# Two levels of seven products in the routed first layers, and first-layer sums that stay in P1's bank and are restored by ScalarE

## The chip, the core and the metric

The kernel runs as one program on one core of a Trainium2 chip. The metric is the device time of one execution in microseconds (us). The kernel before has a median of 1692.92 us over 3 runs (1692.71 to 1692.92). TensorE multiplies matrices, VectorE and ScalarE work on rows of 128 partitions, GpSimd and SyncE (SP) here mostly issue DMAs.

## What is computed

The input x has 2 x 2048 rows of 512 values, in f32 throughout. A modulated linear layer makes z from x. Then z goes through a gated feed-forward layer with a hidden width of 2048: a shared one for all rows, and one of two experts, chosen for each row by its gate score. A row's other expert sees zeros, so that only its biases count.

```python
z = einsum('bsi,io->bso', x * ys[:, None, :], weight) * d[:, None, :]
top1 = argmax(softmax(z @ gate_w.T))
masked = z[None] * one_hot(top1, 2).T[:, :, None]
h = relu(einsum('end,edh->enh', masked, w1) + b1[:, None, :])
routing_output = (einsum('enh,ehd->end', h, w2) + b2[:, None, :]).sum(0)
shared = relu(z @ sw1 + sb1) @ sw2 + sb2
return x + routing_output + shared
```

## The kernel before

**Stages.** The program is one list of stages, and each engine works through its instructions in the order in which the program gives them. The modulation comes first (to about 123 us of the span). Then come four shared units of 1024 rows (loop at L1271), three routed units of 1024 rows that were gathered by expert, one routed unit of 512 rows (loop at L1311), and a last piece of 256 rows (from about 1640 us). A unit (`unit`, L714) has a first layer, 512 to 2048 with relu, and a second layer, 2048 to 512.

**First layer.** Both halves of rows, of inputs and of outputs make 2 x 2 blocks, which are multiplied with seven products in place of eight (Strassen-Winograd): P1 = A11 B11, P2 = A12 B21, P3 = S4 B22, P4 = A22 T4, P5 = S1 T1, P6 = S2 T2, P7 = S3 T3. A are blocks of weights and S their sums, B are blocks of rows and T their sums; T come from `z_sums` (L404), four VectorE operations of the whole width (T3 takes the place of B12). The outputs are h11 = P1+P2, h12 = P1+P6+P5+P3, h21 = P1+P6+P7+P4 and h22 = P1+P6+P7+P5. The loop over c runs 8 times, once for each pair of 128-wide output blocks; `product` (L763) is two matmuls of 128 x 512 in a routed or shared unit. In a pair: P1 goes to a bank and ScalarE copies it to s1 (L779); `last` adds P3 of the pair before to its P5 bank (L804); P6 goes to a bank of its own, and VectorE makes u2 = P6 + s1 (L784); P2 is added in P1's bank and ScalarE's relu reads it (L774); VectorE makes u3 = P7 + u2 (L791), h22 = P5 + u3 (L794) and h21 = P4 + u3 (L798). Banks come from two pools: "pa" and "po".

**Second layer.** `layer2_twice` (L891) uses seven products at two levels: seven calls of `seven` (L916), each of seven products of four 128 x 256 matmuls (L938). The 512-row unit uses one level (`layer2_once`, L827).

**Work put in between.** Hooks name places in a unit: ("in", c) is inside pair c, c behind it, "m0" to "m4" and ("n", step, i) lie in the second layer. `hosted` (L1055) computes a small group of 128 rows inside a routed unit, eight steps of a first part (phr, L1070, 1.75 us of TensorE) and a second (por, L1083). `put` (L1001) transposes finished outputs; `run_late` (L708) calls it step by step. `rows_of` (L391) transposes rows of z in the first shared unit.

**Sums of weights.** The blocks S of the weights are made on VectorE during the shared units and stored in DRAM for later units: for w1 of both experts 16 jobs of `job1` (L263), which load on GpSimd's queue and store to s1E on SP's; for sw2 and w2 twelve jobs of `split_twice` (L278), which load on GpSimd's queue and store on SP's (L293, L303), in pieces of 512 bytes. `split_hooks` (L371) gives 4, 3, 3 and 2 of these jobs to the four shared units. The first shared unit makes sums of sw1 as it goes (`made`, L525); `stored` (L1110) loads blocks and stored sums for a pair of a first layer, two pairs ahead, on SP's queue.

Of the kernel before, what the change touches and what calls it, by code (L numbers as in the profile page):

```python
# [16 lines left out]
def kernel(  # L17
# [36 lines left out]
    P = 128  # L54
# [57 lines left out]
    s1S = dram.tile([1, H2, P, 4, K2, P], F32, name="s1S")  # L112
    s2S = dram.tile([1, 4, P, H2, D // 2], F32, name="s2S")
    s1E = dram.tile([E, H2, P, 4, K2, P], F32, name="s1E")
    s2E = dram.tile([E, 4, P, H2, D // 2], F32, name="s2E")

    H4 = H2 // 2
    LV = ("A11", "A12", "A22", "S1", "S2", "S3", "S4")
    w2S = dram.tile([1, 7, P, 4, H4, P], F32, name="w2S")
    w2E = dram.tile([E, 7, P, 4, H4, P], F32, name="w2E")  # L120

# [31 lines left out]
    b2_sb = wpool.tile([P, D], F32, tag="w1", name="b2_sb")  # L153
    nc.scalar.dma_start(b2_sb[: E + 1, :], b2)
    load_xT(1)
    gate_sb = wpool.tile([P, E, D], F32, tag="w1", name="gate_sb")
# [106 lines left out]
    def job1(e, c):  # L263
        r = work.tile([P, KD, 2, P], F32, tag="cr", name="r1", bufs=2)
        for i in range(2):
            nc.gpsimd.dma_start(
                r[:, :, i, :], w1[e][:, ts(c + i * H2, P)].rearrange("(k p) h -> p k h", p=P)
            )

        def make():  # L270
            o = work.tile([P, 4, K2, P], F32, tag="zp", name="o1")
            lo, hi = slice(0, K2), slice(K2, KD)
            sums([o[:, i] for i in range(4)], r[:, lo, 0], r[:, hi, 0], r[:, lo, 1], r[:, hi, 1])
            nc.sync.dma_start(s1E[e, c], o)

        return make

    def split_twice(todo):  # L278


        def load(src, q, *_):
            r = wpool.tile([P, 4, D], F32, tag="w2", name="jobr")
            nc.gpsimd.dma_start(r, src.rearrange("(j k q p) d -> q p (j k) d", p=P, q=H4, k=2)[q])
            return r

        def group(l0, x, y):

            s2_, s3_, s1_, s4_ = (y[:, l0 : l0 + x(0, 0).shape[1], i] for i in range(4))
            sums((s1_, s2_, s3_, s4_), x(0, 0), x(1, 0), x(0, 1), x(1, 1))

        def keep(dst, q, l0, n, y):
            for i in range(4):
                nc.sync.dma_start(dst[l0 : l0 + n].rearrange("l p m q d -> q m p l d")[q, i], y[:, :, i])  # L293

        held = load(*todo[0])
        yield
        a, b = slice(0, D // 2), slice(D // 2, D)
        for i, (src, q, dst, store, then) in enumerate(todo):
            r = held
            S = wpool.tile([P, 4, 2, D // 2], F32, tag="w2", name="jobs")  # L300
            sums([S[:, i] for i in range(4)], r[:, 0:2, a], r[:, 2:4, a], r[:, 0:2, b], r[:, 2:4, b])
            for k in range(2):
                nc.sync.dma_start(store.rearrange("s p (k q) d -> q k p s d", q=H4)[q, k], S[:, :, k])  # L303
            yield
            for l in (0, 2):
                y = work.tile([P, 2, 4, P], F32, tag="cs", name="y", bufs=2)
                group(0, lambda k, m: S[:, l : l + 2, k, ts(m, P)], y)
                keep(dst, q, 3 + l, 2, y)
            if i + 1 < len(todo):
                held = load(*todo[i + 1])  # L310
            yield
            y = S.rearrange("p s k d -> p (s k d)")[:, : 12 * P].rearrange("p (l m d) -> p l m d", l=3, m=4)
            rj = r.rearrange("p (j k) d -> p j k d", k=2)
            group(0, lambda k, m: rj[:, :, k, ts(m, P)], y)
            group(2, lambda k, m: rj[:, 1:2, k, D // 2 + m * P : D // 2 + (m + 1) * P], y)
            keep(dst, q, 0, 3, y)
            if then:
                yield
                then(q, r)
            yield  # L320
# [32 lines left out]
    class Jobs:  # L353


        def __init__(self, jobs):
            self.jobs, self.make = jobs, None

        def step(self, more=True):
            make, self.make = self.make, (self.jobs.pop(0)() if self.jobs and more else None)  # L360
            if make:
                make()

    expert_jobs = Jobs([lambda e=e, c=c: job1(e, c) for e in range(E) for c in range(H2)])
    split_jobs = [(sw2, q, w2S[0], s2S[0], None) for q in range(H4)]
    for e in range(E):
        split_jobs += [
            (w2[e], q, w2E[e], s2E[e], lambda q, r, e=e: zeros_add(e, q, r)) for q in range(H4)
        ]

    def split_hooks(n):  # L371

        steps = split_twice([split_jobs.pop(0) for _ in range(n)])

        def step():
            for f in zero_late[:]:
                zero_late.remove(f)
                f()
            next(steps, None)

        hooks = {c: [step] for c in range(H2 - 1)}
        hooks.update({("in", c): [step] for c in range(H2 - 1)})
        return hooks
# [20 lines left out]
    def z_sums(W=T):  # L404
        z = [zslot(i, W) for i in range(7)]
        nc.vector.tensor_sub(z[T1], z[B12], z[B11])
        nc.vector.tensor_sub(z[T2], z[B22], z[T1])
        nc.vector.tensor_sub(z[B12], z[B22], z[B12])
        nc.vector.tensor_sub(z[T4], z[B21], z[T2])
# [115 lines left out]
    def made(c):  # L525

        w = wpool.tile([P, 14, P], F32, tag="w1", name=f"w1m_{c}")
        a21 = work.tile([P, K2, P], F32, tag="hs", name=f"a21_{c}", bufs=2)
        nc.sync.dma_start(w[:, 0:4, :], shared_a1(c))
        nc.sync.dma_start(w[:, 4:6, :], shared_a1(c + H2)[:, K2:, :])  # L530
        nc.sync.dma_start(a21, shared_a1(c + H2)[:, :K2, :])

        def make():
            sums([w[:, 6 + 2 * i : 8 + 2 * i] for i in range(4)], w[:, 0:2], w[:, 2:4], a21, w[:, 4:6])
            nc.gpsimd.dma_start(s1S[0, c].rearrange("p s k h -> p (s k) h"), w[:, 6:14])

        return w, make

    first = []
# [174 lines left out]
    def unit(name, W, src, bias, row, hooks, after):  # L714
# [6 lines left out]
        weights, a2, d2, ws, split = src  # L721
# [28 lines left out]
        last = None  # L750
        ws = list(ws) + [weights(c) for c in range(len(ws), 2)]
        for c in range(H2):
            if c == 0:
                ws[0][1]()
            if c + 1 < H2:
                ws[c + 1][1]()
            if len(ws) < min(c + 3, H2):
                ws.append(weights(c + 2))
            w = ws[c][0]

            def product(ps, wi, zi, start, stop, w=w):
                for k in range(K2):
                    nc.tensor.matmul(  # L763
# [5 lines left out]
            def temp(tag):  # L769
                return work.tile([P, W], F32, tag=tag, name=f"{tag}{name}_{c}", bufs=2)  # L770
# [9 lines left out]
            if last is not None:  # L780
                last()
# [609 lines left out]
```

## Time and profile before

| | |
|---|---|
| median of 3 runs | 1692.92 us |
| the profiled execution's time, its span | 1692.93 us, 1691.2 us |
| shared unit 0: first layer, second | 123 to 224 us, 224 to 308 us |
| shared units 1, 2, 3 end at | 497, 689, 876 us |
| routed units of 1024 rows: end at | 1095, 1310, 1522 us |
| routed unit of 512 rows, last piece: end at | 1640, 1691 us |
| DMA, whole run | 335.30 MB, mean 198 GB/s |

The groups of the first layers are the costliest of the page. "r" at the end of a name means routed, "s" shared; two forms are in one group where the 512-row unit's 256-wide tiles are counted too.

```profile
L763 PE MATMUL p1r<-zs_all,w1r 128*128 128x512 f32 (+1 forms) x256 | 106.7, 539 | 0.0
L763 PE MATMUL p5r<-zs_all,w1r 128*128 128x512 f32 (+1 forms) x256 | 106.6, 539 | 0.0
L763 PE MATMUL p1s<-zs_all,w1s 128*128 128x512 f32 x192 | 91.0, 596 | 0.2 <-DVE u3s L791 0.2
```

A row has line, engine and operation, output and inputs, shapes and count; then busy time in us and the mean of one in ns; then the engine's idle time ahead of the group and what ended it. P2 is counted with p1 and P3 with p5, since they share their banks. Rows of "PEld" are weight loads of TensorE, which overlap its matmuls.

### The profile page before, as it was taken

How to read it: one execution, taken by the hardware profiler on the slowest of the kernel's cores; microseconds unless marked ns; L12 is line 12 of the kernel's file. 1: busy time of each engine (PE TensorE's matmuls, PEld its weight loads, DVE VectorE, ACT ScalarE, POOL GpSimd, SP SyncE). 2: the span in 40 equal slices, each digit the busy share in tenths (PEclk: the TensorE clock that was granted, in tenths of full speed). 3: DMA queues.
4: the chain of work that ended last, by engine and by line, in shares of the span. 5: the costliest groups of instructions: out<-in, count | busy, mean ns of one | idle time of the engine just before them, and what ended most of it. 6: DMA issues, size and time to landing. Idle time of an engine off the chain costs nothing. (4 is left out here: it accounts for less than half of the span.)

```text
span 1691.2 us, 18009 instructions
## 1 busy us (share of the span) xinstructions
PE 1678.5 (99%) x6282; PEld 1111.1 (66%) x6282; DVE 1071.1 (63%) x1749; ACT 335.2 (20%) x615; POOL 221.8 (13%) x288
## 2 busy tenths in 40 slices
PE   9999999999999999999999999999999999999998
PEld 4444478655884478545885558855588555888885
DVE  5668879888887879774872238732387322885410
ACT  2333210122002210122022220122201222013110
POOL 1222000120012100131001111002020020201210
PEclk9999999999999999999999999999999999999999
DMA  4759846597656957594634627435374353645661
GB/s 165 283 216 328 273 159 230 189 318 233 219 193 204 360 170 249 187 317 158 222 119 142 201 97 270 143 118 172 125 265 164 103 174 128 208 163 140 238 236 50
DMA packets 239616, 335.30 MB, mean 198 GB/s; under 512 B 17251, under 2 KB 175971, under 8 KB 239014
## 3 DMA queue, kind: packets, MB, share of 16 engines
q1 hardware_dynamic: 210544, 238.41, 42.5%
q0 software_dynamic: 27488, 94.14, 16.5%
q10 hardware_dynamic: 1494, 1.60, 0.3%
q8 instruction: 50, 0.82, 0.2%
q14 instruction: 40, 0.33, 0.1%
HBM read 252.55 MB, written 81.53 MB: 198 GB/s over the span
## 5 line engine op out<-in xcount | busy, mean ns | idle before, releaser
L763 PE MATMUL p1r<-zs_all,w1r 128*128 128x512 f32 (+1 forms) x256 | 106.7, 539 | 0.0
L763 PE MATMUL p5r<-zs_all,w1r 128*128 128x512 f32 (+1 forms) x256 | 106.6, 539 | 0.0
L1235 POOL DMA_INDIRECT out<-ar,idx x33 | 34.9, 1058 | 481.1 <-DVE ar L1234 429.3
L763 PE MATMUL p1s<-zs_all,w1s 128*128 128x512 f32 x192 | 91.0, 596 | 0.2 <-DVE u3s L791 0.2
L791 DVE TENSOR_TENSOR u3r<-p7r,u2r 128x512 f32<-128x512 f32 (+1 forms) x32 | 20.0, 625 | 112.5 <-PE p7r L763 109.9
L763 PE MATMUL p5s<-zs_all,w1s 128*128 128x512 f32 x192 | 90.2, 592 | 0.0
L804 DVE TENSOR_TENSOR h3r<-p5r,u2r 128x512 f32<-128x512 f32 (+1 forms) x32 | 20.0, 624 | 97.5 <-PE p5r L763 97.5
L763 PEld LDWEIGHTS p5r<-zs_all,w1r 128*128 128x128 f32 x256 | 48.6, 190 | 47.5 <-issue 45.9
L763 PEld LDWEIGHTS p1r<-zs_all,w1r 128*128 128x128 f32 x256 | 48.2, 190 | 46.0 <-issue 41.6
L763 PEld LDWEIGHTS p5s<-zs_all,w1s 128*128 128x128 f32 x192 | 36.5, 190 | 45.9 <-issue 43.1
L763 PEld LDWEIGHTS p1s<-zs_all,w1s 128*128 128x128 f32 x192 | 35.3, 190 | 38.2 <-issue 37.5
L1070 PEld LDWEIGHTS phr<-zp,ws 128*128 128x128 f32 x384 | 46.6, 192 | 11.5 <-issue 11.5
L763 PE MATMUL p7r<-zs_all,w1r 128*128 128x512 f32 (+1 forms) x128 | 53.4, 539 | 0.0
L763 PE MATMUL p6r<-zs_all,w1r 128*128 128x512 f32 (+1 forms) x128 | 53.3, 539 | 0.0
L763 PE MATMUL p4r<-zs_all,w1r 128*128 128x512 f32 (+1 forms) x128 | 53.3, 539 | 0.0
L1229 POOL DMA_INDIRECT ar<-accD,idx x33 | 34.6, 1048 | 141.1 <-PE pst L1165 129.2
L938 PE MATMUL S1s<-zs_all,w2s 128*128 128x256 f32 x224 | 52.9, 379 | 0.0
L938 PE MATMUL S2s<-zs_all,w2s 128*128 128x256 f32 x224 | 52.9, 379 | 0.0
L938 PE MATMUL a22s<-zs_all,w2s 128*128 128x256 f32 x224 | 52.9, 379 | 0.0
L413 POOL DMA_DIRECT2D zs_all<-zTD x16 | 11.5, 728 | 281.4 <-PE S1s L938 270.1
L1105 POOL DMA_DIRECT2D accD<-xr x32 | 17.8, 557 | 227.1 <-DVE xr L1104 225.3
L774 ACT ACTIVATE h3s<-h3s,b_sb 128x512 f32<-128x512 f32 x32 | 23.1, 722 | 120.8 <-DVE h3s L804 120.8
(421 smaller groups left out, 3573.9 us busy)
## 6 DMA issues: line engine op xcount, KB each, us to landing
ws<-w SPq DMA_DIRECT2D x48, 512.0 KB, 8.0
w2s<-w2S SPq DMA_DIRECT2D x28, 768.0 KB, 6.0
w1r<-s1E SPq DMA_DIRECT2D x32, 512.0 KB, 5.5
w2r<-w2E SPq DMA_DIRECT2D x21, 768.0 KB, 6.3
w1s<-s1S SPq DMA_DIRECT2D x24, 512.0 KB, 6.4
zTD<-zt POOLq DMA_DIRECT2D x8, 1024.0 KB
zD<-zr POOLq DMA_DIRECT2D x32, 256.0 KB
zs_all<-zTD POOLq DMA_DIRECT2D x16, 512.0 KB
```

What stands on the lines that cost most here:

```text
L413: nc.gpsimd.dma_start(zslot(slot), zTD[u][:, k : k + K2, t : t + T])
L763: nc.tensor.matmul(ps, w[:, wi + k, :], zslot(zi, W)[:, k, :], start=(start and k == 0), stop=(stop and k == K2 - 1), skip_group_check=not ...
L774: nc.scalar.activation(o, i, AF.Relu, bias=bias[:, hc : hc + 1], scale=1.0)
L791: nc.vector.tensor_add(u3, p7, u2)
L804: nc.vector.tensor_add(h12[:, c, :], p5, u2)
L938: nc.tensor.matmul(ps, w[m][:, c, :], x.of[m][:, c, :], start=(start and c == 0), stop=(c == H4 - 1), skip_group_check=not start,)
L1070: nc.tensor.matmul(ph[:, ts(i, P)], w[:, k * W + i * P : k * W + (i + 1) * P], zt[:, k, :], start=(k == 0), stop=(k == KD - 1),)
L1105: nc.gpsimd.dma_start(accD[ts(c, P), :], xr)
L1229: nc.gpsimd.indirect_dma_start(out=ar, out_offset=None, in_=accD[:, :], in_offset=at)
L1235: nc.gpsimd.indirect_dma_start(out=out[:, :], out_offset=at, in_=ar, in_offset=None)
```

## The change

- A routed unit of 1024 rows gets a new first layer, `layer1_twice`: seven products at two levels. It has 14 steps (seven outer products, each for two halves g of the output blocks), and a step has seven products of two 128 x 256 matmuls, which fill the two halves of one bank. Its operand sums come from `quarter_sums`, its weights from a new DRAM store w1E, loaded in two parts per step, two steps ahead. VectorE adds each step's outputs to those of earlier steps; relus are handed out up to four a step from step 9 on, and twelve stand at the end. Hosted work, transposes of outputs and the sums of z are handed out over the steps by `more`, `run_late` and `give`.
- The other units keep one level (`layer1_once`), with another order: P1's bank is kept for P6, P7 and P4, which are added in it; ScalarE copies the running sum to s1, u2 and u3 instead of VectorE adding it; ScalarE then puts P1 back from s1 into the bank, and P2 is added.
- The jobs on weights become 20 of one kind: four on sw2, eight on w1 of both experts, eight on w2, five in each shared unit. Their loads move from GpSimd's queue to SP's. The stores are laid out by quads of blocks, in pieces of 4 KB. The 512-row unit makes its sums of w1 as it goes.

The core of the diff, with lines left out at "...":

```diff
+    w1E = dram.tile([E, H4, P, 7, 7, P], F32, name="w1E")
+    w2S = dram.tile([1, H4, P, 7, 4, P], F32, name="w2S")
+    w2E = dram.tile([E, H4, P, 7, 4, P], F32, name="w2E")
...
-    def job1(e, c):
-        r = work.tile([P, KD, 2, P], F32, tag="cr", name="r1", bufs=2)
-        for i in range(2):
-            nc.gpsimd.dma_start(
-                r[:, :, i, :], w1[e][:, ts(c + i * H2, P)].rearrange("(k p) h -> p k h", p=P)
-            )
...
+    def job_w1(e, q):
+        def load(r):
+            for c in range(KD):
+                nc.sync.dma_start(
+                    r[:, c].rearrange("p (g h) -> p g h", h=P),
+                    w1[e][ts(c, P), :].rearrange("p (g q h) -> q p g h", g=4, q=H4)[q],
+                )
+        def keep(l0, n, y):
+            nc.sync.dma_start(w1E[e, q, :, l0 : l0 + n, 1:5], y)
+        def keep_parts(l0, n, x):
+            to = w1E[e, q, :, l0 : l0 + n]
+            nc.sync.dma_start(to[:, :, 0], x(0, 0)[:, :, :P])
+            nc.sync.dma_start(to[:, :, 5:7].rearrange("p l m h -> p l (m h)"), x(1, 0))
+        return load, q, lambda l, S: None, keep, keep_parts, None
...
+    split_jobs = [job_w2(sw2, q, w2S[0], s2S[0], None) for q in range(H4)]
+    split_jobs += [job_w1(e, q) for e in range(E) for q in range(H4)]
...
+    def quarter_sums(t, x):
+        Q = x.shape[2] // 2
+        b11, b12, b21, b22 = x[:, 0, :Q], x[:, 0, Q:], x[:, 1, :Q], x[:, 1, Q:]
+        nc.vector.tensor_sub(t[:, 0], b12, b11)
+        nc.vector.tensor_sub(t[:, 1], b22, t[:, 0])
+        nc.vector.tensor_sub(t[:, 2], b22, b12)
+        nc.vector.tensor_sub(t[:, 3], b21, t[:, 1])
...
-            s1, u2, u3 = temp("s1"), temp("u2"), temp("u3")
-            p1 = half_bank("pa", f"p1{name}_{c}")
-            product(p1, 0, B11, True, True)
-            nc.scalar.copy(s1, p1)
-            if last is not None:
-                last()
-            p6 = half_bank("pa", f"p6{name}_{c}")
-            product(p6, 8, T2, True, True)
-            nc.vector.tensor_add(u2, p6, s1)
-            product(p1, 2, B21, False, True)
-            relu(h11[:, c, :], p1, 0)
...
+                def p1(self):
+                    self.product(self.b1, "A11", B11, True)
+                    nc.scalar.copy(self.s1, self.b1)
+                def p1_again(self):
+                    nc.scalar.copy(self.b1, self.s1)
+                def p2(self):
+                    self.product(self.b1, "A12", B21)
+                    self.relu(h11[:, self.c, :], self.b1, 0)
+                def p5(self):
+                    self.b5 = half_bank("po", f"p5{name}_{self.c}")
+                    self.product(self.b5, "S1", T1, True)
+                def p6(self):
+                    self.product(self.b1, "S2", T2)
+                    nc.scalar.copy(self.u2, self.b1)
+                def p7(self):
+                    self.product(self.b1, "S3", B12)
+                    nc.scalar.copy(self.u3, self.b1)
+                def c22(self):
+                    nc.vector.tensor_add(h22[:, self.c, :], self.b5, self.u3)
+                def p4(self):
+                    self.product(self.b1, "A22", T4)
+                    self.relu(h21[:, self.c, :], self.b1, 1)
+                def p3(self):
+                    self.product(self.b5, "S4", B22)
+                    nc.vector.tensor_add(h12[:, self.c, :], self.b5, self.u2)
...
+                pair = Pair(c)
+                pair.p1()
+                if c < H2 - 1:
+                    pair.p5()
+                if before:
+                    before.p4()
+                    before.p1_again()
+                if c == H2 - 1:
+                    pair.p2()
+                    pair.p1_again()
+                    before.p2()
+                    for f in hooks.get(("in", c), ()):
+                        f()
+                    pair.p6()
+                    before.p3()
+                    pair.p7()
+                    pair.p5()
+                    pair.c22()
+                else:
+                    pair.p6()
+                    for f in hooks.get(("in", c), ()):
+                        f()
+                    if before:
+                        before.p3()
+                        before.p2()
+                    pair.p7()
+                    pair.c22()
...
-            p7 = half_bank("pa", f"p7{name}_{c}")
-            product(p7, 10, B12, True, True)
-            nc.vector.tensor_add(u3, p7, u2)
-            p5 = half_bank("po", f"p5{name}_{c}")
-            product(p5, 6, T1, True, True)
-            nc.vector.tensor_add(h22[:, c, :], p5, u3)
-            relu(h22[:, c, :], h22[:, c, :], 1)
-            p4 = half_bank("pa", f"p4{name}_{c}")
-            product(p4, 4, T4, True, True)
-            nc.vector.tensor_add(h21[:, c, :], p4, u3)
-            relu(h21[:, c, :], h21[:, c, :], 1)
...
+            plan = [
+                ("A11", B11, h11, None), ("S2", T2, h12, h11), ("S3", B12, h21, h12), ("S1", T1, h22, None),
+                ("A12", B21, h11, h11), ("A22", T4, h21, h21), ("S4", B22, h12, h12),
+            ]
+            steps = [(j, g) for j in range(7) for g in range(2)]
...
+            def load(n):
+                j, g = steps[n]
+                wa, wb, then = weights(LV.index(plan[j][0]), g)
+                ws.append((wa, wb))
+                wb_later.append(then)
...
+                def product(self, ps, m, start=False):
+                    k = PARTS.index(m)
+                    w = self.w[k // 4]
+                    for i in range(2):
+                        nc.tensor.matmul(
+                            halves_of(ps)[:, i], w[:, i, k % 4], self.x.of[m],
+                            start=(start and i == 0), stop=True, skip_group_check=True,
+                        )
...
+                def out2(self, i, b, u):
+                    if self.base:
+                        plus(self.o[i], halves_of(u), self.base[i])
+                        plus(self.o[i], halves_of(b), self.o[i])
+                    else:
+                        plus(self.o[i], halves_of(b), halves_of(u))
+                def p1(self):
+                    self.product(self.b1, "a11", True)
+                    nc.scalar.copy(self.s1, self.b1)
+                def p2(self):
+                    self.product(self.b1, "a12")
+                    if self.base:
+                        plus(self.o[0], halves_of(self.b1), self.base[0])
+                    else:
+                        nc.scalar.copy(self.o[0], halves_of(self.b1))
+                def p5(self):
+                    self.b5 = bank("po", f"S1{name}_{self.n}")
+                    self.product(self.b5, "S1", True)
+                def p6(self):
+                    self.product(self.b1, "S2")
+                    nc.scalar.copy(self.u2, self.b1)
+                def p7(self):
+                    self.product(self.b1, "S3")
+                    nc.scalar.copy(self.u3, self.b1)
+                    self.out2(3, self.b5, self.u3)
+                def p4(self):
+                    self.product(self.b1, "a22")
+                    if self.base:
+                        t = work.tile([P, W], F32, tag="cs", name=f"c{name}_{self.n}", bufs=2)
+                        nc.scalar.copy(t, self.b1)
+                        plus(self.o[2], halves_of(t), self.base[2])
+                    else:
+                        nc.scalar.copy(self.o[2], halves_of(self.b1))
+                    nc.scalar.copy(self.b1, self.s1)
+                def p3(self):
+                    self.product(self.b5, "S4")
+                    self.out2(1, self.b5, self.u2)
...
+                def end(self):
+                    g = self.g
+                    relus.extend(later)
+                    later.clear()
+                    done = {3: (h22, 1), 4: (h11, 0), 5: (h21, 1), 6: (h12, 0)}.get(self.j)
+                    if self.j == 3:
+                        for o, x in ((h12, h22), (h22, h21)):
+                            for m in range(2):
+                                at = slice(m * H4 + 2 * g, m * H4 + 2 * g + 2)
+                                adds.append(lambda o=o[:, at], x=x[:, at]: plus(o, o, x))
+                    if done:
+                        h, half = done
+                        for c in (2 * g, 2 * g + 1, H4 + 2 * g, H4 + 2 * g + 1):
+                            later.append(lambda c=c: nc.scalar.activation(
+                                h[:, c, :], h[:, c, :], AF.Relu,
+                                bias=bias[:, c + half * H2 : c + half * H2 + 1], scale=1.0,
+                            ))
...
+            first_sums = z_sums(W, False)
+            x = Operand1(0, box.pop("t"))
+            before = None
+            for n, (j, g) in enumerate(steps):
+                if 2 < n + 2 < len(steps):
+                    load(n + 2)
+                step = Step(n, x)
+                step.p1()
+                step.p5()
+                if before:
+                    before.p4()
+                step.p6()
+                give(adds, 2)
+                if n == len(steps) - 1:
+                    give(x1.sums, 1)
+                more()
+                if n == 0:
+                    give(first_sums, 2)
+                if n == len(steps) - 1:
+                    before.p3()
+                    step.p7()
+                    before.p2()
+                else:
+                    if before:
+                        before.p3()
+                        before.p2()
+                    step.p7()
+                give(wb_later, 1)
+                give(relus, 4)
+                give(adds, 2)
+                if n == 0:
+                    give(first_sums, 2)
+                else:
+                    run_late(1)
+                if g == 1:
+                    x = x_next
+                elif j < 6:
+                    x_next = Operand1(j + 1)
+                if before:
+                    before.end()
+                if n == len(steps) - 2:
+                    give(x1.sums, 2)
+                more()
+                before = step
+            before.p4()
+            before.p3()
+            before.p2()
+            give(x1.sums, 1)
+            before.end()
+            give(relus + later, 12)
...
+            def weights(l, g):
+                src = w1E[one, 2 * g : 2 * g + 2, :, l].rearrange("e c p m h -> p (e c) m h")
+                wa, wb = pair_tiles(f"r{k}_{l}_{g}")
+                wa, wb = (w.rearrange("p (c m) h -> p c m h", c=2) for w in (wa, wb))
+                nc.sync.dma_start(wa, src[:, :, 0:4])
+                return wa, wb, lambda: nc.sync.dma_start(wb, src[:, :, 4:7])
+            return weights
```

## Prediction

> **What bounds the kernel now.** I read the page first (part 1), then who waited for whom on TensorE, then the busy time by stretches cut at the stages, then the groups with shapes kept apart, then the timeline for spacings.
>
> The page, part 1 (busy us, share of the span, instructions):
>
> ```profile
> span 1691.2 us, 18009 instructions
> PE 1678.5 (99%) x6282; PEld 1111.1 (66%) x6282; DVE 1071.1 (63%) x1749; ACT 335.2 (20%) x615; POOL 221.8 (13%) x288
> ```
>
> TensorE is busy 99% of the span. Its waits sum to 5.8 us; these two are the longest (us in total, times, longest):
>
> ```profile
> PE S1s L938 <- DVE c0s L968: 1.3, 1, 1.3
> PE p1s L763 <- ACT s1s L779: 1.2, 1, 1.2
> ```
>
> So every matmul taken away counts in full until another engine can't follow. Stretches (us, then PE, PEld, DVE, ACT, POOL busy with counts, PE clock, DMA share, GB/s): shared unit 0's first layer, routed unit 0's first layer, its second.
>
> ```profile
> 125.00:223.00 98.00, 96.51 (x252) 44.57 (x251) 76.95 (x207) 31.34 (x49) 11.85 (x20) 1.00 0.94 297
> 876.00:1007.00 131.00, 130.94 (x433) 69.35 (x434) 41.75 (x60) 32.78 (x60) 8.78 (x16) 1.00 0.41 134
> 1007.00:1095.00 88.00, 87.86 (x425) 77.27 (x424) 73.27 (x90) 10.71 (x27) 15.18 (x12) 1.00 0.65 219
> ```
>
> The clock is full throughout (1.00). ScalarE is nearly free in the routed first layer (32.8 of 131 us), where the change puts it to work. Groups by shape (busy us, mean ns):
>
> ```profile
> L763 PE MATMUL p1r<-zs_all,w1r 128*128 128x512 f32 x192 | 90.2, 592 | 0.0
> L779 ACT COPY s1r<-p1r 128x512 f32<-128x512 f32 x24 | 14.1, 586 | 62.7 <-PE p1r L763 53.5 <-DVE zs_all L408 9.2
> L774 ACT ACTIVATE h1r<-h1r,b1p 128x512 f32<-128x512 f32 x24 | 17.3, 722 | 83.5 <-DVE h1r L794 83.5
> L784 DVE TENSOR_TENSOR u2r<-p6r,s1r 128x512 f32<-128x512 f32 x24 | 16.6, 690 | 23.0 <-PE p6r L763 23.0
> ```
>
> A PE row's mean overlaps its neighbour's, so I price matmuls by spacing in the timeline (start us, us):
>
> ```profile
> 754.73 1.88 PE L763 MATMUL p5s<-zs_all,w1s 128*128 128x512 f32 x4
> 756.45 1.88 PE L763 MATMUL p6s<-zs_all,w1s 128*128 128x512 f32 x4
> ...
> 790.78 1.89 PE L938 MATMUL a11s<-h0s,w2s 128*128 128x256 f32 x8
> 792.51 1.89 PE L938 MATMUL S1s<-zs_all,w2s 128*128 128x256 f32 x8
> ```
>
> Each f32 matmul is two records. Over 20 products from 754.73 to 789.06 a product of two 512-wide matmuls takes 1.7165 us, so one takes 0.858; over 42 products from 790.78 to 863.30 one of four 256-wide takes 1.7267, so one takes 0.432.
>
> Latencies:
>
> ```profile
> 126.93 0.58 ACT L779 COPY s1s<-p1s 128x512 f32<-128x512 f32 x1
> 127.57 1.99 PE L763 MATMUL p1s<-zs_all,w1m 128*128 128x512 f32 x4 [1.20 <-ACT s1s L779]
> 129.39 1.91 PE L394 MATMUL pt<-ident,zt 128*128 128x128 f32 x16
> 129.59 0.69 ACT L774 ACTIVATE h0s<-p1s,b_sb 128x512 f32<-128x512 f32 x1 [2.08 <-PE p1s L763]
> ...
> 136.63 0.72 ACT L774 ACTIVATE h1s<-h1s,b_sb 128x512 f32<-128x512 f32 x1 [2.17 <-DVE h1s L794]
> 137.26 0.71 ACT L774 ACTIVATE h2s<-h2s,b_sb 128x512 f32<-128x512 f32 x1
> ```
>
> A copy ending at 127.51 lets TensorE start at 127.57: 0.06 us. That product then needs 1.82 instead of 1.72 until the next starts: 0.1 lost per refill. ScalarE starts 0.20 us after a product's stream gives way to the next (129.39 to 129.59). Two relus follow each other at 0.63. So product, copy, product on one bank needs 0.20 + 0.585 + 0.06 = 0.845 us between the two products.
>
> **The change part by part.**
>
> *Matmuls.* A routed unit of 1024 rows has 8 x 7 x 2 = 112 matmuls of 512 columns in its first layer. After: 14 steps x 7 x 2 = 196 of 256. Three units: -336 x 0.858 + 588 x 0.432 = -288.4 + 253.8 = -34.6 us. Nothing else on TensorE changes in count: shared units and the 512-row routed unit keep seven products, reordered.
>
> *ScalarE instead of VectorE.* u2 and u3 become copies of the running sum, and P1 is put back by a copy. ScalarE gets 270 copies of 512, 24 of 2x256 and 24 of 256 columns more: 294 x 0.585 + 24 x 0.37 = 181 us, 335 to about 516 of some 1660: no bound on average. VectorE loses 216 PSUM adds in first layers (149 us of 0.69 each) and gets 204 adds of 2x256, 24 of 1024 (1.22), 84 quarter sums (0.42) and the larger weight sums: about +90 us net, 70% busy. Both lie beside TensorE; what counts is where TensorE waits on the new chain. A put-back from SBUF into PSUM is in no row. Nearest are the 0.586 copy out of PSUM and the 0.722 relu within SBUF, which also reads a bias. ScalarE: Activation LUTs, of the Trainium skill (Step-by-step), holds that ScalarE reaches PSUM sooner than SBUF. I take 0.6, ends 0.5 and 0.8.
>
> PSUM — Partial Sum Buffer, of the skill (its summary of rules for kernel authors), speaks against putting P1 back: a sum started by ScalarE should start from zero on this chip, any other value going in through TensorE. The same page says that a matmul does add to a written value where an earlier one has marked the element, which P1's has; no run shows it here. By the rule each put-back would be an identity matmul: 42 + 32 of 512 columns at 0.858 and 8 of 256 at 0.432, 67 us, and the sum would end near 1744, slower. By the rows it is a copy beside TensorE, at no time of its own, as long as two products lie between; that is what I sum.
>
> *Waits in a routed step*, T=0 at its first product, q=0.863. The order is p1(n) p5(n) p4(n-1) p6(n) p3(n-1) p2(n-1) p7(n); ScalarE's is s1(n), the two copies of p4(n-1), u2(n), u3(n), then up to four relus. p6 starts at 2.59, s1 is done at 1.65: slack 0.9. p4 ends at 2.59, its two copies end near 3.9, p2 starts at 4.32: slack 0.4. u2 ends near 4.5, p7 starts at 5.18: slack 0.7. VectorE's two adds of a step's S3 product end 2.2 us after p7, and p3, which adds into the bank they read, starts 3.4 after it: slack 1.2. (The eight adds of 1024 columns fall in steps 8 and 9, where hosted work of 1.7 us follows p6 or p7; without it they would cost up to 2 us there.) A bank is used again by transposes or a later step only when a full step has passed since its last reader was queued, so I count nothing for that. A plain step thus runs at TensorE's pace. Five places don't:
> - First step: p7 directly follows p6: 0.845 + 0.1 = 0.95.
> - Step 12: four relus after u3(11) and no hosted work behind p7(11). u3, relus and s1(12) end 3.84 after p7(11); p6(12) could start at 2.59: 1.31 + 0.1 = 1.4.
> - Step 11: hosted work (1.75) covers, but its two relus (0.36) also come ahead: 0.25.
> - Step 13: u2 behind two copies: 0.25.
> - End: the put-back of step 13 stands behind four relus. It ends at 9.8, p3 at 8.0: 1.9.
>
> Together 4.8 a unit, 14.4 for three. The twelve relus left for the end reach the second layer: they end about 6.6 us after its start, ahead of its own first copy, which is needed only after five products (8.6): nothing.
>
> *Waits in one-level first layers.* Products of 1.72 us halve the density, so steady pairs never wait. Only the first pair has p7 right behind p6: 0.95 in three shared units (transposes fill it in unit 0), about 1.0 with a tail wait in the 512-row unit: 3.9. Unit 0's first copy is late already (the 1.2 above); its order gives 0.2 more.
>
> *Weight sums, loads, stores.* Jobs leave GpSimd's queue for SP's. There each store waits for VectorE with the weight loads behind it, needed two pairs (24 us) later. SP already waits this way (it loses 123.5 us to the same stores) without TensorE noticing. VectorE's own add that frees a bank for p3 has 6.9 us of products to hide in, more than the longest job step put ahead of it (2.8). Sixteen small jobs on w1 become eight large: written bytes grow by 17 MB, routed loads by 16.5 MB, the 512-row unit saves 3: 335 to about 366 MB. A routed step loads 0.9 MB and its share of hosted weights, near 190 GB/s; the second layer ran at 219 without a stall. Loads are issued two steps (17 us) ahead; the like landed in 5.5 us. I take zero, ends -1 and +8, since shared unit 0 already stands at a DMA share of 0.94, though its 512-byte stores become 4 KB ones.
>
> **Sum.** The profiled execution took 1692.93, its span 1691.2, the median 1692.92: the same to 0.01. 1692.9 - 34.6 + 14.4 + 3.9 + 0.2 = 1676.8, say 1677.
>
> **Rivals.**
> - *The full gain.* ScalarE keeps up everywhere: 1692.9 - 34.6 = 1658, in practice 1660 to 1668 as the first-step waits are structural. For it: ScalarE has under 6 us of work in most steps. Against: it works in order, and the relus stand ahead of copies. 0.17.
> - *Every routed step waits.* With 0.8 for the put-back and a copy that starts late, slacks of 0.4 turn into waits of 0.25 at 42 steps: +10, 1684 to 1689. Against: the rows of copies are narrow (562 to 587). 0.19.
> - *Slower: weights late in the routed first layers.* SP's queue is in order and each step's second load waits for a product of the step before. If a step's 0.9 MB and the hosted 1 MB land only at a rate under about 170 GB/s (1.5 MB in 9 us), each step waits; from 0.5 us a step (42 x 0.5 = 21) the time is over 1696. For it: the bytes per step, in pieces of 1.5 to 2 KB. Against: 297 GB/s in a stretch of before. 0.06.
> - *Nothing left.* Stalls eat the 34.6 within 3.4 us: 0.05.
>
> **How the numbers follow.** The forecast's own case, 1669 to 1684, has 0.53. I leave out the lower part of the full gain (0.06) and the last two rivals (0.11), 0.17 in all: 1663 to 1689. The unknown costs of the put-back and of the loads lie within it. A difference under 0.2% (3.4 us) can't be told from none. Faster 0.89, same 0.05, slower 0.06.
>
> **What would show it.** PE busy falls to about 1644; 588 more matmuls of 256, 336 fewer of 512; ScalarE near 516 us; TensorE's waits near 20 us, first for ScalarE's u2 at first steps, s1 and the put-back at steps 12 and 13. A spread of equal waits at every step says the second rival; waits for DMA in routed first layers the third. I am wrong if TensorE waits for VectorE (sums of operands, adds of bases), which I count at nothing because they lead by a step.

## The result, and the profile after

The changed kernel takes 1679.95 us (median of 4 runs, 1679.12 to 1680.43); the kernel before took 1692.92 (4 runs, 1692.71 to 1693.55). The ratio is 0.9922, with a 95% interval of 0.9905 to 0.9939. The forecast was 1677. The profiled execution took 1680.43 us, its span is 1678.7, against 1692.93 and 1691.2 before: 12.5 us less.

Part 1 of the page of after:

```profile
span 1678.7 us, 19747 instructions
PE 1650.3 (98%) x6786; PEld 1203.4 (72%) x6786; DVE 1159.9 (69%) x1949; ACT 495.0 (29%) x933; POOL 190.4 (11%) x252
```

TensorE is busy for 28 us less with 504 more matmul records; VectorE went from 1071 to 1160 us, ScalarE from 335 to 495. The waits of TensorE, longest sums first (us in total, times, longest):

```profile
PE S1r L1005 <- DVE h3r L1015: 4.2, 3, 1.4
PE a11r L1005 <- ACT s1r L1021: 3.0, 3, 1.0
PE p1s L847 <- ACT u2s L873: 2.0, 3, 0.7
PE a11r L1005 <- ACT u2r L1036: 2.0, 3, 0.7
PE p5r L847 <- DVE wam L194: 1.4, 1, 1.4
...
PE p1s L847 <- DMA was<-sw: 0.5, 1, 0.5
```

All that are listed sum to 19.2 us, in before to 6.1. "3 times" is once for each of three units: every stall has one place in a unit. None of them is a wait for weights of a routed unit.

Where the time went is best read from the start of the first product of each stage in the timeline (us):

| stage | before | after | difference | forecast |
|---|---|---|---|---|
| modulation | 122.77 | 122.63 | -0.1 | 0 |
| shared units 0 to 3 | 756.91 | 760.37 | +3.5 | +3.05 |
| first layers of the three routed units of 1024 | 382.99 | 362.11 | -20.9 | -20.2 |
| their second layers | 264.31 | 264.31 | 0.0 | 0 |
| unit of 512 rows | 101.16 | 103.92 | +2.8 | +1.0 |
| last piece, to the end of the span | 63.03 | 65.32 | +2.3 | 0 |

The span fell by 12.5 us, 3.6 less than the 16.1 of the forecast: the last two rows are 4.1 us worse, the shared units 0.4, and the routed first layers 0.7 better.

In the first layer of routed unit 0 (columns as in the stretches of before) every engine but TensorE has more to do in less time, and TensorE still sets the pace. Before's stretch in the prediction is 131.0 us; the layer itself took 127.67 of it.

```profile
883.00:1003.70 120.70, 117.55 (x585) 97.31 (x584) 77.52 (x119) 60.08 (x112) 12.80 (x19) 1.00 0.61 200
```

### The profile page after: what moved, and what is told of

It is laid out like the page before. It is cut to its first block, busy times and chain, and to the rows that moved or that the text cites. A ratio compares the mean times of both kernels' runs of the same rounds, so it can differ in the third digit from the quotient of the medians.

```text
span 1678.7 us, 19747 instructions
## 1 busy us (share of the span) xinstructions
PE 1650.3 (98%) x6786; PEld 1203.4 (72%) x6786; DVE 1159.9 (69%) x1949; ACT 495.0 (29%) x933; POOL 190.4 (11%) x252
## 2 busy tenths in 40 slices
DMA packets 287370, 366.08 MB, mean 218 GB/s; under 512 B 18404, under 2 KB 218596, under 8 KB 287271
## 5 line engine op out<-in xcount | busy, mean ns | idle before, releaser
L847 PE MATMUL p1s<-zs_all,was 128*128 128x512 f32 x288 | 135.7, 596 | 2.5 <-ACT u2s L873 2.0
L847 PEld LDWEIGHTS p1s<-zs_all,was 128*128 128x128 f32 x288 | 52.9, 190 | 63.2 <-issue 56.2
L847 PE MATMUL p1s<-zs_all,wbs 128*128 128x512 f32 x192 | 89.2, 592 | 0.0
L1005 PE MATMUL a11r<-tr,war 128*128 128x256 f32 x288 | 74.6, 381 | 3.3 <-ACT s1r L1021 3.0
L1005 PEld LDWEIGHTS a11r<-tr,war 128*128 128x128 f32 x288 | 54.0, 190 | 13.1 <-ACT s1r L1021 4.2
L1005 PE MATMUL S1r<-zs_all,wbr 128*128 128x256 f32 x168 | 43.5, 381 | 4.2 <-DVE h3r L1015 4.2
L1405 PE MATMUL phr<-zp,ws 128*128 128x128 f32 x384 | 46.8, 275 | 0.0
L1273 PEld LDWEIGHTS a22s<-zs_all,w2s 128*128 128x128 f32 x224 | 42.6, 190 | 5.8
L847 PE MATMUL p1s<-zs_all,wam 128*128 128x512 f32 x96 | 44.6, 595 | 1.2 <-ACT s1s L858 1.2
L470 POOL DMA_DIRECT2D zs_all<-zTD x16 | 11.5, 728 | 301.7 <-PE S1s L1273 220.6
L847 PE MATMUL p5s<-zs_all,wbs 128*128 128x512 f32 x96 | 45.2, 593 | 0.0
```

The source lines that it names most:

```text
L470: nc.gpsimd.dma_start(zslot(slot), zTD[u][:, k : k + K2, t : t + T])
L847: nc.tensor.matmul(ps, self.w[l][:, k, :], zslot(zi, W)[:, k, :], start=(start and k == 0), stop=(k == K2 - 1), skip_group_check=not start,)
L1005: nc.tensor.matmul(halves_of(ps)[:, i], w[:, i, k % 4], self.x.of[m], start=(start and i == 0), stop=True, skip_group_check=True,)
L1273: nc.tensor.matmul(ps, w[m][:, c, :], x.of[m][:, c, :], start=(start and c == 0), stop=(c == H4 - 1), skip_group_check=not start,)
L1405: nc.tensor.matmul(ph[:, ts(i, P)], w[:, k * W + i * P : k * W + (i + 1) * P], zt[:, k, :], start=(k == 0), stop=(k == KD - 1),)
```

## Experiments

"Changed" is the kernel after the change. Stage times are from each run's trace. Those of the routed units repeat to 0.1 us where nothing was changed in them; the modulation and a single shared unit vary by up to 1.5 us between runs. "By spacing" means from the starts of TensorE's matmuls: how much later one starts than the matmul ahead of it, at its usual pace, would have it. That is more than the wait which the profile names, since the first product after a wait is slower too.

### Do the two levels make the gain?

```diff
-            if n < U:
+            if n <= U:
...
-        if k < NLARGE:
+        if k < 0:
...
-            k < NLARGE,
+            False,
```

> The routed units of 1024 rows take one level (in the order that keeps P1's bank), with sums of w1 made as they go; the stored sums of w1 are still made in the shared units. If the two levels are what gains (my theory: 34.6 us of matmuls less, about 14 us of waits more), the first layer of each of the three routed units goes back from 120.7 us to before's 127.7 plus 0.95 for its first pair, 128.6, and the kernel ends near 1680 + 3 x 7.9 = 1704, 11 us above before. Rival: the gain comes from the other parts (fewer adds on VectorE, stores in larger pieces), then it stays under 1693.

Measured: 1708.21 us (ratio to before 1.0092, 1.0075 to 1.0109), span 1706.2. The three first layers took 129.8, 131.5 and 129.8 us, 1.2 to 2.9 more than expected. The first pair's 0.95 did not come, since hosted matmuls lie between its P6 and P7. In its place TensorE waits at the start of each layer for the first sums of w1, which VectorE makes late, 2.13 us by spacing (the four waits are three routed units of 1024 and the one of 512):

```profile
PE p5r L847 <- DVE wam L194: 7.0, 4, 1.9
```

In the second of these units TensorE's granted clock is 0.50 for 3.41 us after that wait, which loses 1.7 us more (131.5 against 129.8); in the other two the same wait is not followed by it. The stretch in the trace (the columns behind the busy times are the clock, the DMA share and GB/s):

```profile
1105.32:1108.73 3.41, 3.41 (x5) 1.35 (x4) 2.51 (x6) 0.00 (x0) 0.00 (x0) 0.50 0.02 7
```

Of the 29.0 us that the three layers are longer, 6.4 are these waits and 1.7 the clock; the other 20.9 us, 3 x 6.97, are what two levels save against one. So the two levels are the gain, and all of it. Without them the other parts leave the kernel slower than before, also without that wait (here with the sums of w1 that are still stored and no longer used).

### The end of a routed first layer

Two edits, the second on top of the first. Lines with `relus` are the first edit, those with `x1.sums` (VectorE's sums for the second layer) the second.

```diff
-                if n == len(steps) - 1:
-                    give(x1.sums, 1)
...
-                give(relus, 4)
+                give(relus, 4 if n < len(steps) - 1 else 0)
...
-            give(x1.sums, 1)
+            give(x1.sums, 2)
...
-            give(relus + later, 12)
+            give(relus + later, 16)
```

The relus alone:

> The four relus that stand before the last put-back of P1 in a routed unit move behind it. As the prediction put it, the put-back behind four relus is the whole cause of the wait at the end: TensorE gets back about 1.7 us a unit, 5 us in all, 1675. Rival, from the trace of after: the S4 product there waits for VectorE's adds that read P5's bank (1.39 us), and its end coincides with that of the put-back, so that nothing is gained: within 0.5 us, 1680.

Measured: 1679.53 us (0.9923, 0.9907 to 0.994). Each first layer is 0.16 us shorter, not 1.7. With VectorE's sum moved too:

> As the run with the relus moved, and VectorE's third operand sum of the second layer (1.22 us) moves behind the last products as well. If VectorE and ScalarE end together at the end of the first layer, both moves together gain 1.1 us a unit, 3.3 us, near 1676.5. If only the relus matter, the same as with the relus alone. If only VectorE matters, the relus move alone gives nothing and this gives the same 1.1 a unit, which the two runs can't tell apart from the first case, but the start of the last product after the put-back can.

Measured: 1678.3 us (0.9914, 0.9898 to 0.9931). Each first layer is 1.12 us shorter, and each second layer 0.60 longer, since its first copy now stands behind sixteen relus and TensorE waits for it:

```profile
PE a11r L1271 <- ACT s1r L1292: 1.0, 3, 0.3
```

The timeline of after at this place shows why one edit alone gives nothing (start us, us):

```profile
997.71 1.22 DVE L823 TENSOR_TENSOR zs_all<-h0r 128x1024 f32<-128x1024 f32 x1
...
999.03 2.56 ACT L1071 ACTIVATE h2r<-h2r,b1p 128x512 f32<-128x512 f32 x4
...
1000.96 0.69 DVE L1015 TENSOR_TENSOR h3r<-S1r,h3r 128x512 f32<-128x512 f32 x1
...
1001.70 1.13 PE L1005 MATMUL S1r<-zs_all,wbr 128*128 128x256 f32 x4 [1.39 <-DVE h3r L1015]
1002.09 0.59 ACT L1051 COPY a11r<-s1r 128x512 f32<-128x512 f32 x1
...
1002.73 1.13 PE L1005 MATMUL a11r<-zs_all,wbr 128*128 128x256 f32 x4
```

S4 starts when VectorE has read P5's bank (1001.65); P2 behind it starts at 1002.73. The put-back ends at 1002.68. Two chains end at once, and the view of waits names only the first: the second has no row of its own. VectorE's sum was not moved alone; by these lines the put-back would then still hold P2.

### Step 12

```diff
                 step.p1()
+                if n == 12:
+                    give(relus, 4)
                 step.p5()
...
-                give(relus, 4)
+                give(relus, 0 if n == 11 else 4)
```

> Only the four relus between step 11 and step 12 move, behind the copy s1 of step 12, where hosted matmuls follow. Theory: the 1.28 us before P6 of step 12 go (1.17 waiting and 0.11 of refill) and nothing else comes: 3.8 us in three units, 1676. Rival: the relus then delay the put-back of step 11 and the wait moves to P2, gain under 1 us.

Measured: 1675.64 us (0.9903, 0.9886 to 0.9919). Each first layer is 1.27 us shorter, 119.43. In after, s1 of step 12 stands behind the relus; here it goes first, and hosted matmuls cover the relus. ScalarE in after, then in the run:

```profile
982.68 2.56 ACT L1071 ACTIVATE h0r<-h0r,b1p 128x512 f32<-128x512 f32 x4
985.14 0.56 ACT L1021 COPY s1r<-a11r 128x512 f32<-128x512 f32 x1
```

```profile
981.45 0.59 ACT L1021 COPY s1r<-a11r 128x512 f32<-128x512 f32 x1 [0.33 <-PE a11r L1005]
981.93 2.56 ACT L1071 ACTIVATE h0r<-h0r,b1p 128x512 f32<-128x512 f32 x4
```

### The first step and the first pair

```diff
-                upto = min(len(beside), len(beside) * state[0] // (2 * len(steps) - 2))
+                upto = min(len(beside), max(1, len(beside) * state[0] // (2 * len(steps) - 2)))
...
+                    else:
+                        ahead = Pair(1)
+                        ahead.p1()
                     pair.p7()
```

> Something is put between P6 and P7 of the first step or pair: in routed units of 1024 rows the first hosted matmuls, elsewhere P1 of the second pair. Theory: the copy u2 is the only cause of the wait there; each of three routed units gains 0.95 to 1.03, each of three shared units 0.95, the unit of 512 rows 0.7: 6.5 us, near 1673.5. Rival: P7 is held by its weights or by the first sums on VectorE too, and less than half of it comes back.

Measured: 1674.04 us (0.9889, 0.9872 to 0.9905). Each routed first layer is 0.94 us shorter, the first layers of shared units 1 to 3 together 2.99, the unit of 512 rows 0.73. Shared unit 0, where transposes fill the place already, loses 0.5. In the routed units the copy u2 behind P6 was the cause, to a hundredth of the forecast 0.95, and in shared unit 3 it gave back 0.92. Shared units 1 and 2 gave 0.44 and 1.64; unchanged, their first layers vary by 0.3 and 1.5 between runs, so only the sum of the three bears on it.

### How much the put-back has to spare

```diff
+                    nc.scalar.copy(self.s1, self.s1)
                     nc.scalar.copy(self.b1, self.s1)
```

> One more ScalarE copy of 512 columns (0.59 us, of s1 onto itself) ahead of each put-back in the routed units of 1024 rows. If each step's put-back has 0.4 us to spare, as the prediction has it for a plain step, 39 steps wait by 0.2 to 0.3 and it ends near 1690. If hosted matmuls between P6 and P2 cover most steps, as the trace of after shows, only the four or five steps without them wait, 0.45 each, and the last 0.6: about 7 us, 1687. No change would say that ScalarE isn't near the path at all.

Measured: 1688.23 us (0.9973, 0.9964 to 0.9982; 11 runs, 1686.43 to 1689.98); each routed first layer is 2.46 us longer. By spacing, 0.36 each is lost at four steps without hosted work (1, 5, 9, 10), the rest at step 13 and the end. Here at step 5, where P2 starts 0.25 us later than TensorE's pace:

```profile
926.62 1.03 PE L1005 MATMUL S1r<-zs_all,wbr 128*128 128x256 f32 x4
927.73 1.13 PE L1005 MATMUL a11r<-zs_all,wbr 128*128 128x256 f32 x4
```

In after, the put-back of this step ends 0.31 us before P2 starts, and TensorE needs 0.06 of that: 0.25 to spare. The extra copy ends it 0.5 us later (copies overlap a little), so P2 waits 0.25, and 0.1 more goes in the slower product behind the wait. So the put-back is near the path in four plain steps. In the others, by sum, the 1.75 us of hosted matmuls come on top: 2 us to spare.

### The price of a put-back through TensorE

```diff
-                    nc.scalar.copy(self.b1, self.s1)
...
                 def p2(self):
+                    nc.tensor.matmul(self.b1, ident, self.s1, start=True, stop=True)
                     self.product(self.b1, "a12")
```

> P1 is put back by TensorE, a matmul of the identity with s1 that starts the sum anew, ahead of each P2, instead of by ScalarE's copy: 42 + 32 of 512 columns and 8 of 256. By the prediction's price 67 us more on TensorE, less about 1 us a unit where the put-back was late: 1743 to 1747, slower than before by 50. Rival: f32 matmuls by the identity hide in waits, and it costs under half of that.

This kernel leaves out the put-back of the last pair in the five one-level first layers, where P6 follows it and not P2; P6 then adds onto P1 + P2. That makes 70 matmuls of 512 columns and 7 of 256, 63.1 us by the prediction's prices. Measured: 1738.36 us (1.0271, 1.0254 to 1.0288), 58.4 above the changed kernel. The "67 us" of the expectation had the last pairs in it. A shared first layer grew by 5.3 to 6.0 us (7 x 0.858 = 6.0), a routed one by 11.15 (14 x 0.858 = 12.0, less a stall).

### What the one-level layers get from their new order

The edit puts before's loop over c in place of the pairs; at P6, for one:

```diff
-                    self.product(self.b1, "S2", T2)
-                    nc.scalar.copy(self.u2, self.b1)
...
+                product(p6, "S2", T2, True, True)
+                nc.vector.tensor_add(u2, p6, s1)
```

> The one-level first layers (shared units and the unit of 512 rows) get back before's order and VectorE adds, all else as changed. Theory: staying in P1's bank gains nothing there and costs the first pair's 0.95 in three shared units and 1.1 in the unit of 512 rows: 1680 - 3.9 = 1676. Rival: with ten adds more a pair on VectorE, beside the larger sums of weights, TensorE waits for VectorE in the shared units, and it is slower than 1680 by several us.

Measured: 1704.24 us (1.0073, 1.0051 to 1.0096; 1701.07 to 1709.46), 24 us slower than the changed kernel. The shared units grew by 7.4, 4.9, 6.4 and 3.2, the unit of 512 rows by 1.1. VectorE does three more adds a pair (u2, u3 and h21; not ten). TensorE waits for u2 and u3, which the new order leaves to ScalarE, and for the add of h22 (h1s here), which stands behind u3:

```profile
PE p1s L848 <- DVE u3s L876: 9.5, 6, 4.7
PE p5s L848 <- DVE h1s L879: 5.1, 3, 2.5
...
PE pos L1296 <- DVE u2s L869: 2.5, 1, 2.5
```

My theory fell. What keeps these adds? The longest wait, in shared unit 1:

```profile
381.82 0.69 DVE L194 TENSOR_TENSOR jobs<-jobr 128x512 f32<-128x512 f32 x1 [3.83 <-DMA w1E<-jobs]
...
384.67 0.68 DVE L876 TENSOR_TENSOR u3s<-p7s,u2s 128x512 f32<-128x512 f32 x1
...
385.41 3.65 PE L848 MATMUL p1s<-zs_all,was 128*128 128x512 f32 x4 [4.71 <-DVE u3s L876]
```

A job on weights stands ahead of u3 in VectorE's queue, and it first waits 3.83 us for a store of earlier sums. In unit 2 such a wait is 5.89 us; in unit 3 and at most places of unit 0 the sums of weights themselves fill the time ahead of the adds. In the changed kernel VectorE waits for such stores too (3.0 us in unit 1), and TensorE doesn't wait there.

Part of the loss is the clock. TensorE's granted clock is 0.50 in three stretches behind such waits, 3.41, 6.83 and 3.41 us long (shared units 1 and 2, the unit of 512 rows), which is about 6 us of time; in unit 0 it is 1.00 throughout. Above, four matmul records take 3.65 us in place of 1.88.

Is it VectorE's load, or that the adds stand on the path? The other run keeps the changed kernel and adds work of the same length that nobody waits for:

```diff
                     nc.scalar.copy(self.u2, self.b1)
+                    self.spare(2)
...
+                def spare(self, n):
+                    for i in range(n if W == T else 0):
+                        t = work.tile([P, 256], F32, tag="spare", name=f"spare{name}_{self.c}_{n}_{i}")
+                        nc.vector.tensor_add(t, self.s1[:, :256], self.s1[:, :256])
```

> As changed, with five adds of 256 columns (0.42 us each, 2.1 us) more on VectorE in each pair of the shared units' first layers, read by nobody: the work of the three adds of 512 (3 x 0.69) that before's order does more a pair. If VectorE's load is what made the run with before's order slower (6 to 7 us in a shared unit), most of it comes back here: 15 to 23 us, 1695 to 1703. If it is that TensorE waits on those very adds for banks, it costs under 8 us.

Measured: 1692.06 us (0.9993, 0.9985 to 1.0002), 12 us slower than the changed kernel, between the two expectations. Shared units 0 and 3 grew by 4.6 and 6.2, units 1 and 2 by nothing that shows. TensorE waits once in unit 3 (for `part`, a sum over weights of an expert) and once in unit 0:

```profile
PE pcr L387 <- DVE part L381: 3.1, 1, 3.1
...
PE p5s L847 <- DVE h1s L887: 2.6, 1, 2.6
```

The clock falls at both, to 0.50 for 3.41 us and for 6.83 us:

```profile
205.31:208.71 3.40, 3.40 (x6) 1.33 (x5) 3.33 (x12) 0.00 (x0) 0.00 (x0) 0.50 0.95 277
782.16:788.98 6.82, 6.43 (x14) 3.21 (x15) 6.05 (x16) 0.00 (x0) 1.07 (x2) 0.50 0.39 155
```

That loses about 1.7 and 3.2 us: nearly half of what the spare adds cost. Shared unit 0's first layer in after, with before's order, and with the spare adds (the columns after the length are PE, PEld, DVE, ACT, POOL):

```profile
125.00:223.00 98.00, 96.80 (x252) 44.53 (x251) 70.88 (x206) 42.30 (x71) 11.97 (x22) 1.00 0.93 330
```

```profile
125.00:223.00 98.00, 90.34 (x235) 41.19 (x234) 81.92 (x223) 28.32 (x47) 11.95 (x22) 1.00 0.88 313
```

```profile
125.00:223.00 98.00, 94.20 (x242) 43.02 (x241) 83.00 (x240) 39.87 (x67) 11.97 (x22) 0.98 0.89 311
```

With the spare adds VectorE is as busy as with before's order (83.0 and 81.9 of 98 us). TensorE's busy time can't be compared, since at clock 0.50 the same matmul is busy for longer (mean clock 0.98 in the third row); its waits can: 2.6 us in unit 0 against 6.5 with before's order, and 5.7 against 18.5 in all four units. So both count. The load alone makes TensorE wait in units 0 and 3, and the place of the adds on the path, behind jobs that wait for stores, is what these two runs leave for units 1 and 2. How much is which can't be split further: the waits fall at other places, the clock adds to both, and the spare adds are not quite without effect (ScalarE once waits 1.3 us for one of them, which reads s1).

### All mends together

The edits of the end, of step 12 and of the first step (not in shared unit 0), and one more:

```diff
-        return {"m2": [do], "m4": [first_make]} if make else {"m2": [do]}
+        return {"m2": [do], "m3": [first_make]} if make else {"m2": [do]}
```

> All that the runs so far point to, together: the relus of step 11 behind s1 of step 12 (3.8 us), something between P6 and P7 of first steps and pairs, not in shared unit 0 (2.8 in routed units, 3.0 in shared ones, 0.7 in the unit of 512 rows), relus and VectorE's sum behind the last products (3.4 in first layers less 1.8 given back in second layers), and the first sums of w1 for the unit of 512 rows one place of the second layer earlier (1.5). If the waits are independent: 1680 - 13.4 = 1666.5. Rival: with one wait gone the next is late by about as much, and it stays above 1671.

Measured: 1666.38 us (5 runs, 1665.5 to 1667.57), ratio to before 0.9844, 0.983 to 0.9857. A routed first layer takes 117.4 us (3.34 less, 0.94, 1.27 and 1.12 by the runs above), its second layer 0.6 more than in after, and the unit of 512 rows 2.4 less. The waits were independent; this version beats both kernels.

## Why the prediction held, and where it did not

*Matmuls, -34.6.* Right. In the run with all mends a routed first layer takes 117.4 us and its spacing still shows 1.2 of stalls, so 116.2 without them: 11.5 less than before's 127.67, and 34.6 / 3 = 11.53.

*Waits in a routed unit, 4.8.* The sum is 11.53 - 6.96 = 4.57. By spacing: first step 1.03 (forecast 0.95), step 12 1.28 (1.4), step 13 0.36 (0.25), step 11 nothing (0.25), end 1.83 (1.9). Edits made for the cause gave back the first step (0.94) and step 12 (1.27) in the forecast size; of the end they gave back 1.12, and the second layer lost 0.60 of that again.

*"End: the put-back of step 13 stands behind four relus."* Right in size and only half the cause, so that the size was in part luck. I followed ScalarE's queue there and not VectorE's, where a 1.22 us sum of the second layer stands ahead of the two adds that free P5's bank. Removing my cause alone gave 0.16 us.

*One-level first layers, 3.9.* The first pairs cost what was said (2.99 came back in the three shared units, of which unit 3 alone is clear of their variation), and the unit of 512 rows its 1.1. What I did not list there: its first sums of w1 are made behind the last product of the unit before, and S1 T1 waits for them, 1.7 us by spacing. I counted how long VectorE's sums take and not when the first one is due.

*VectorE "beside TensorE".* The number was right, and the reason I gave was incomplete. I priced the new order by its costs alone. The run with before's order shows what it pays for: behind the larger jobs on weights, VectorE's adds on the path cost some 24 us, about 6 of them by the clock. The prediction should have asked what cover the removed adds give to the added sums.

*Slack of 0.4 in each plain step.* It is 0.25 in four steps and about 2 by sum in the others, where hosted matmuls lie between P6 and P2. That is why the rival "every routed step waits" did not come, and a copy more ahead of each put-back costs 2.46 a unit, not 4.

*ScalarE at 516 us.* It was 495: copies that follow each other start about 0.5 us apart (985.14, 985.60 in after) and overlap in the records, whose durations sum to 528. TensorE's busy time is 1650 rather than 1644, since part of each stall is counted as busy: a routed first layer loses 4.5 us by spacing, of which 3.1 are listed as waits. With all mends the busy time is 1645.4.

*Weights, loads and stores at zero.* Right: one wait for a DMA of 0.5 us, in a shared unit. A first part of the routed weights lands in 5.3 us, in before its like in 5.5, and the kernel moves 366.08 MB, as forecast.

*The end of the span, 2.3 us.* Not foreseen. From the last scatter on, SP waits longer for TensorE's sequencer (here the longest is 3.5 us, before 0.9), and one packet of an instruction queue lands there:

```profile
SPq L1750 <- PEq L1750: 4.0, 2, 3.5
```

All variants of the changed kernel have a last piece of 65.3 us, those with other numbers of matmuls too. What is fetched, and why, stays open; it was not tried.

## What to carry to other kernels

When sums move from one engine to an in-order neighbour, write out that neighbour's queue at the ends of a stage and wherever batched work is handed out: here the middle of the stage had cover, and the ends had not. A wait in a profile names the chain that ended last, and a second one may end 0.05 us earlier; look for it before you price the mend. Before you call a run slower by what was changed in it, look whether the clock fell behind one of its waits. And price a change that relieves an engine together with what the same change loads on it.

## What the runs showed of the hardware

ScalarE's copy from SBUF into PSUM takes as long as one out of PSUM. The third row, from the run with the extra copy, is one that stays within SBUF:

```profile
L1051 ACT COPY a11r<-s1r 128x512 f32<-128x512 f32 x42 | 24.8, 590 | 1.3
L1040 ACT COPY u3r<-a11r 128x512 f32<-128x512 f32 x42 | 24.6, 586 | 68.4 <-PE a11r L1005 68.4
...
L1051 ACT COPY s1r<-s1r 128x512 f32<-128x512 f32 x42 | 26.2, 623 | 0.0
```

ScalarE: Activation LUTs, of the Trainium skill (Step-by-step), has PSUM as the nearer port for it; with the source in SBUF the rows agree, by 33 of 623 ns. PSUM — Partial Sum Buffer, of the skill (The four PSUM rules), would have a value other than zero put in by a matmul with the identity, or added after the sum has left the bank. No row shows the state of a bank, so the runs give its price alone: 58.4 us for 77 of the 82 put-backs, against 0.59 us copies beside TensorE.

A stall costs more than its wait: the 1.01 us before P6 of step 12 are 1.28 by spacing, 1.17 until P6 starts and 0.11 since P6 itself takes 0.97 until the next starts, in place of 0.863.

It can cost more still. At six of TensorE's waits, of 1.9 to 4.7 us, in three of these runs, the granted clock falls to 0.50 for 3.41 or 6.83 us; at five others in these runs, of 1.8 to 2.5 us, it stays at 1.00. In before, in after and with all mends no wait between 20 us and the last matmul is longer than 1.4 us, and the clock stays at 1.00 over that time. What decides between the two was not tried.
